# A graph-network kernel: prologue reordered, gathers three groups ahead, 32 instead of 20 rows left for the node stage

## The chip, the cores and the metric

The kernel runs on one core of a Trainium2 chip. The metric is the device time of one execution in microseconds (us), the median of several. A hardware profile of a single execution of the kernel before is used beside it. Engines are called as the profile calls them: PE (matrix products; PEld is its weight load), DVE (vector work), ACT (activations and copies), POOL (here the engine that issues the indirect DMAs), SP (here only an issuer of DMAs). "ACTq" and "SPq" stand for DMAs issued by those engines.

## What is computed

Two graph layers over 6250 nodes with 128 features and 100000 edges; `dst` is sorted, `src` is random.

```
radial = exp(coeff * (edge_weight - offsets)**2)                       # 50 per edge
h   = silu(concat(x[src], x[dst], radial) @ Wm1 + bm1)
h   = silu(h @ Wm2 + bm2);  messages = h @ Wm3 + bm3
out = segment_sum(messages, dst)
u   = silu(concat(x, out) @ Wu1 + bu1) @ Wu2 + bu2
x   = layernorm(x + silu(u @ Wi1 + bi1) @ Wi2 + bi2)

xt  = logmap0(x);  xs = xt[src]
att = sigmoid(concat(xs, xt[dst], edge_attr_128) @ att_w.T + att_b)
s   = xt + segment_sum(xs * att, src) + mean(edge_attr_128, src) + mean(edge_attr_128, dst)
out = layernorm(x + proj(expmap0(s)))
```

The means over `src` need every row of edge_attr_128 (100000 x 128) brought from the order of `dst` into the order of `src`.

## The kernel before

Edges go in 98 groups (`NG`) of 1024 edges; a group has 8 rows of 128 edges (b = 0 to 7), and two halves of 4 rows each. Nodes go in 49 blocks (`NB`) of 128. All of it is in `window_path` (L603).

**Prologue** (L874 to L1052). `x` is loaded in three chunks of blocks 0-8, 8-24 and 24-49, three SP DMAs each (L888 to L892). `src` and `dst` go into the tile `raw` by six DMAs from ACT's queue (L893 to L896). Small constants follow from POOL's queue (L897), then zero fills of table ends from SP (L900 to L902), and DVE clears `acc[:, 1]` (L903); DVE has cleared the end of `xs` before (L882). Then come two passes (`s` = 0 and 1) of 13 rounds of four node blocks (L1021). In pass 0 PE transposes `x` (L1014), ACT copies the result to SBUF (L1015), PE multiplies with the sources' part of Wm1 (L1033), DVE copies that to `pj_sb` (L1037), and SP writes it to the table `p_src` in HBM (L1044). Pass 1 does the same with the destinations' part for `p_dst`, and there ACT copies (L1039) and clears a piece of `acc` beside each of the first eight rounds (L1017). `pj_sb` has three buffers (L1030). Small pieces of index work (the list `pieces`, L992) are issued one a round from the fourth round of pass 0 on: turn `src` and `dst` to edge-per-partition form (`turn`, L928 to L930), the windows' bases (`bases`, `spread`, L941 to L953), positions relative to the bases (`relative`, L958, written to HBM at L960), high and low parts of the indices. What is left is issued after the rounds, then `lower(0)` and `lower(1)` (L989, L990; an ACT cast and a DMA from ACT's queue each). At the start of pass 1, SP issues the loads of groups 0 and 1 (L1023 to L1025).

**Edge stage** (L1282 to L1324). Each group needs 8 indirect DMAs by POOL that gather rows of `p_src` (`gather`, L1080, the DMA at L1087) into a tile `ga`, of which there are four (L836), and up to four loads of 64 rows of `p_dst` (`load_rows`, L1078, SP). The gathers of two groups are issued before the loop, and in the loop every half issues four of the group two further on (L1301). For each half, PE transposes the gathered rows and multiplies (L1204, L1207), ACT applies silu (L1210), PE and ACT do the second layer (L1219, L1221, L1223), PE sums the messages and the edge attributes by destination (L1236, L1238, L1240), and DVE adds to `acc` (L1252). DVE also works out, for each edge, its slot in a table ordered by source (`place`).

**Rows of edge_attr.** Rows 0, 1 and 2 of each group are scattered early into the table `early` by POOL's indirect DMAs (`scatter`, L816, the DMA at L818): two of the three rows of a group in the edge stage, straight after the half's gathers (L1302), as soon as ACT has written an index into the rows (L1324, the last thing of the group before). Row g % 3 of a group, the "third row", is always left for the node stage. `left(g)` (L550) names one more row to leave, in every fifth group, 20 in all; `early(g, half)` (L543) says which row a half scatters, if any. Rows 3 to 7 go in the attention stage.

**Node stage** (L1337 to L1473). The update of the nodes, 13 turns of four blocks. Beside it the left rows are moved: `middle` (L1337) holds 33 entries with the 98 third rows and 7 with the 20 left rows. `move_middle` (L1342) does one entry: load its rows again (SP, L1353), set an index by ACT (one copy for three rows at a constant stride, L1356, or one for each row, L1359), scatter them (POOL, L818). It is called three times in each of the 13 turns (L1425), and for the entries that are left after the turns (L1473). SP and POOL run in the order in which the program lists their work. The four tiles that it uses (L1353) are those that the first attribute loads of the attention stage use.

**Attention stage.** Summing by source (L1519 to L1829), with the late rows' scatters and the reads of the table `early` (`bucket_load`, L1590).

Of the kernel before, what the change touches and what calls it, by code (L numbers as in the profile page):

```python
# [8 lines left out]
F32 = mybir.dt.float32  # L9
I32 = mybir.dt.int32  # L10
AF = mybir.ActivationFunctionType
OP = mybir.AluOpType
# [4 lines left out]
P = 128  # L17
# [531 lines left out]

def left(g):  # L550

    return (1, 2, 0)[g % 3] if g % 5 == 0 else None

# [49 lines left out]
def window_path(ctx, tc, bad, x, src, dst, edge_attr, edge_weight, Wm1, bm1, Wm2, bm2, Wm3, bm3,  # L603
                Wu1, bu1, Wu2, bu2, Wi1, bi1, Wi2, bi2, att_w, att_b, out):
    nc = tc.nc
    ordered = ExitStack()
    ordered.enter_context(tc.manual_schedule())
    N, F = x.shape
    E = src.shape[0]
    NB = (N + P - 1) // P  # L610
    NFULL = N // P
    NREM = N - NFULL * P
    ROWS = 50 * P
# [3 lines left out]
    GE = 4 * WE  # L617
# [33 lines left out]
    row_rel = dram.tile([NG, GE], BF16, name="row_rel")  # L651


    const = ctx.enter_context(tc.tile_pool(name="const", bufs=1))
    ident = const.tile([P, P], F32, name="ident")
    make_identity(nc, ident)
# [34 lines left out]

    noff = const.tile([P, 1], F32, name="noff")
    nc.vector.tensor_scalar(noff, part, -float(KR), -STEP, op0=OP.add, op1=OP.mult)


    waiting = []
# [73 lines left out]
    later(attb, att_b[None, :].to_broadcast([P, 1]))  # L770


    keep = ctx.enter_context(tc.tile_pool(name="keep", bufs=1))

    src_i = sent.tile([P, 8, NG], I32, name="src_i")
    rel = sent.tile([P, 8, NG], F32, name="rel")
    hif = keep.tile([P, 2, 8, NG], F32, name="hif")
# [3 lines left out]
    first = sent.tile([P, 8, NG], F32, name="first")  # L781
    base_i = keep.tile([1, NG, 4], I32, name="base_i")
    badc = keep.tile([P, 1], F32, name="badc")
    acc = keep.tile([P, 3, ROWS], F32, name="acc")
    nc.vector.memset(ew3, 0.0)
    nc.vector.memset(badc, 0.0)

# [45 lines left out]

    of_edges = ExitStack()
    eload = of_edges.enter_context(tc.tile_pool(name="eload", bufs=2, reuse_waits="tile"))
    egat = of_edges.enter_context(tc.tile_pool(name="egat", bufs=4, reuse_waits="tile"))  # L836
    attrs, ids = {}, {}

    def extent(g):
# [34 lines left out]
    with tc.tile_pool(name="init", bufs=1) as init, \  # L874
            tc.tile_pool(name="initw", bufs=3) as initw, \
            tc.tile_pool(name="initp", bufs=2, space=PSUM) as initp:

        xs = acc[:, 0, :NB * F].rearrange("p (r f) -> p r f", f=F)
        xT = acc[:, 2, :NB * P].rearrange("f (r p) -> f r p", p=P)
        XL = N - (P - 1) * NB  # L880
        xv = x[:(P - 1) * NB].rearrange("(p r) f -> p r f", r=NB)
        nc.vector.memset(xs[96:, XL:], 0.0)  # L882
        raw = init.tile([NG, 2, GE], I32, name="raw")
        R0 = 96
        assert R0 == NG - 2 and NG * GE - E < GE
        nc.gpsimd.iota(raw[R0:, 0, TAIL:], pattern=[[1, GE - TAIL]], base=N, channel_multiplier=0)
        nc.vector.memset(raw[R0:, 1, TAIL:], -1)
        for lo, hi in ((0, 8), (8, 24), (24, NB)):  # L888
            nc.sync.dma_start(xs[:112, lo:hi], xv[:112, lo:hi])
            nc.sync.dma_start(xs[112:P - 1, lo:hi], xv[112:, lo:hi])  # L890
            nc.sync.dma_start(xs[P - 1:, lo:min(hi, XL)],
                              x[(P - 1) * NB + lo:(P - 1) * NB + min(hi, XL)][None])  # L892
        for s, v in enumerate((src, dst)):  # L893
            nc.scalar.dma_start(raw[:R0, s], v[:R0 * GE].rearrange("(g e) -> g e", e=GE))
            nc.scalar.dma_start(raw[R0:NG - 1, s], v[None, R0 * GE:(NG - 1) * GE])
            nc.scalar.dma_start(raw[NG - 1:, s, :TAIL], v[None, (NG - 1) * GE:])  # L896
        for f in waiting:  # L897
            f()
        for t in (p_src, p_dst):
            nc.sync.dma_start(t[NB * P:], zrow[:, :F])  # L900
        nc.sync.dma_start(first_t[(NB - 1) * LO:NB * LO].rearrange("(p r) f -> p r f", p=P),
                          zrow[:, None, :RW].to_broadcast([P, LO // P, RW]))  # L902
        nc.vector.memset(acc[:, 1], 0.0)  # L903


        rawf = init.tile([NG, 2, GE], F32, name="rawf")
# [11 lines left out]
        def turn(s):  # L918

            for h in range(2):  # L920
                pi = initp.tile([P, 4, P], F32, name="pi")
                for j in range(4):
                    k, c = divmod(4 * h + j, 2)
                    nc.tensor.transpose(
                        pi[:, j, :NG],
                        rawf[:, s].rearrange("g (k p c) -> g k c p", k=4, c=2)[:, k, c],
                        ident[:NG, :NG])
                nc.vector.tensor_copy((src_i, dst_i)[s][:, 4 * h:4 * h + 4], pi[:, :, :NG])  # L928
                if s:
# [32 lines left out]
        def upper(s):  # L962
            nc.vector.tensor_single_scalar(ti, (src_i, dst_i)[s], 7, OP.arith_shift_right)
            nc.vector.tensor_copy(hif[:, s], ti)
# [21 lines left out]
        def lower(s):  # L986
# [2 lines left out]
            nc.scalar.copy(rb, raw[:, s].rearrange("g (k p c) -> g k c p", k=4, c=2))  # L989
            nc.scalar.dma_start(row_lo[:, s], rb.rearrange("g k c p -> g (k c p)"))  # L990

        pieces = [  # L992
            lambda: nc.vector.tensor_copy(rawf[:, 0], raw[:, 0]),
            lambda: turn(0),
            lambda: nc.vector.tensor_copy(rawf[:, 1], raw[:, 1]),
            lambda: nc.vector.tensor_reduce(mx, dw, AX.X, OP.max),
            least,
            lambda: nc.vector.tensor_reduce(base, gone, AX.X, OP.min),
            bases, spread, relative, lambda: turn(1), lambda: upper(0), lambda: upper(1), rest, begins,
            lambda: bias_rows(init, bm2x, bm2p),  # L1000
            lambda: nc.vector.tensor_copy(beside[:, 1:], attw),
            copy_lws,
            lambda: nc.vector.tensor_single_scalar(raw, raw, P - 1, OP.bitwise_and)]


        tabs = [t[:NB * P].rearrange("(p r) f -> p r f", r=NB) for t in (p_src, p_dst)]
# [13 lines left out]
        turn_x(0)  # L1020
        for s in range(2):  # L1021
            if s:
                load(0)  # L1023
                load_attr(0)
                load(1)  # L1025
            for r, (b0, nb) in enumerate(rounds):
                if s == 0:
                    turn_x(r + 1)
                if r % 2 == 0:
                    pj_sb = initw.tile([P, 8, F], F32, name="pj_sb")  # L1030
                pj = initp.tile([P, 4, F], F32, name="pj")
                for i in range(nb):
                    nc.tensor.matmul(pj[:, i], lhsT=xT[:, b0 + i], rhs=wm1n[:, s],  # L1033
                                     start=True, stop=True)
                at = b0 % 8
                if s == 0:
                    nc.vector.tensor_copy(pj_sb[:, at:at + nb], pj[:, :nb])  # L1037
                else:
                    nc.scalar.copy(pj_sb[:, at:at + nb], pj[:, :nb])  # L1039
                    if r < 8:  # L1040
                        clear_sums.pop(0)()
                if r % 2 or r == len(rounds) - 1:
                    lo = b0 - at
                    nc.sync.dma_start(tabs[s][:, lo:lo + at + nb], pj_sb[:, :at + nb])  # L1044
                if s or r >= 3:
                    for _ in range(1):
                        if pieces:
                            pieces.pop(0)()
        for p_ in pieces:
            p_()  # L1050
        for s in range(2):
            lower(s)  # L1052

# [4 lines left out]
    with tc.tile_pool(name="ework", bufs=2, reuse_waits="tile") as ework, \  # L1058
# [3 lines left out]
            tc.tile_pool(name="eslot", bufs=1, reuse_waits="tile", space=PSUM) as eslot:  # L1062
        gas, feats, hots, hid1, hid2, sums, his = ({} for _ in range(7))

        counts = ework.tile([P, 2, NB], F32, name="counts", bufs=1)
        nc.vector.memset(counts, 0.0)
        befores = [ework.tile([P, 10, NB], BF16, name=f"before{i}", bufs=1) for i in range(2)]
# [12 lines left out]
        def gather(g, bs):  # L1080
            if g >= NG:
                return
            if g not in gas:
                gas[g] = egat.tile([P, 8, F], F32, name="ga")
            for b in bs:
                if b < 2 * windows(g):
                    nc.gpsimd.indirect_dma_start(  # L1087
                        out=gas[g][:, b], out_offset=None, in_=p_src[:, :],
                        in_offset=bass.IndirectOffsetOnAxis(ap=src_i[:, b, g:g + 1], axis=0))
# [189 lines left out]

        load_rows(0)  # L1280
        load_rows(1)
        for g in range(2):  # L1282
            gather(g, range(8))
        prepare(0, 0)
        rank(0)
# [3 lines left out]
        for g in range(NG + 2):  # L1289
            for half in range(2):  # L1290
                i = 2 * g + half
                if half == 0 and g + 2 < NG:
                    load_rows(g + 2)
                if half == 0 and g + 2 < NG:
                    load(g + 2)
                if half == 0 and g + 1 < NG:
                    load_attr(g + 1)

                if clear and i % 4 == 0:
                    nc.sync.dma_start(*clear.pop(0))  # L1300
                gather(g + 2, range(4 * half, 4 * half + 4))  # L1301
                if g < NG and early(g, half) is not None:  # L1302
                    scatter(g, early(g, half), attrs[g][0][:, early(g, half)])
                layer1(i)
                if i in extra:
                    extra[i]()
                layer2(i - 1)
                for f in clear_sums[:3]:
                    f()
                del clear_sums[:3]  # L1310
                add_up(i - 3)
                if g < NG and half == 0:
                    hot_of(g)
                if g + 1 < NG:
                    prepare(g + 1, half)
                    if half:
                        place(g + 1)
                if g < NG and half == 1:
                    weigh(g)
                sum_up(i - 2)  # L1320
                if g + 1 < NG and half == 0:
                    rank(g + 1)
                if g + 1 < NG and half == 1:
                    nc.scalar.copy(attrs[g + 1][0][:, :, F + 2], lof[:, :3, g + 1])  # L1324
# [548 lines left out]
```

## Time and profile before

| | |
|---|---|
| median of 6 runs | 2859.98 us (2857.42 to 2874.05) |
| the profiled execution | 2867.95 us, span 2866.1 us, mean granted PE clock 0.739 |
| PE / PEld busy | 1965.7 us (69%) / 1717.2 us (60%) |
| DVE busy | 1663.3 us (58%) |
| ACT busy | 914.2 us (32%) |
| POOL busy | 1528.1 us (53%) |
| DMA | 412.10 MB, mean 144 GB/s |
| gathers of `p_src` (L1087) | 782, 751.8 us busy, 961 ns each |
| early scatters in the edge stage (L818) | 176, 176.2 us busy, 1001 ns each |

The span is the profiled time from the first to the last recorded instruction; 1.9 us of the execution lie outside of it. In a list of instructions the columns are: start in us, duration in us, engine, line, operation, output<-input, shape, count, and in brackets the idle time of the engine before it and what ended that ("<-issue": nothing that the profile shows). In a table by stretches of time the columns are the stretch, its length, then the busy time and the number of instructions of PE, PEld, DVE, ACT and POOL, the granted PE clock (1.00 is full), the share of the DMA engines that was busy, and GB/s.

### The profile page before, as it was taken

The page shows a single profiled execution, that of the slowest core. Times are in us where ns is not written, and L with a number is a line of the kernel's source. Part 1 is how long each engine was busy: PE and PEld are TensorE (multiplying, and loading weights), DVE is VectorE, ACT ScalarE, POOL GpSimd, SP SyncE. Part 2 cuts the span into 40 slices and gives each one's busy share as a digit, 9 for nine tenths or more (in the row PEclk, how much of TensorE's full clock was granted, in tenths as well). Part 3 has the DMA queues.
Part 4 walks back from the last instruction along what each step waited for, and adds up shares of the span by engine and source line. Part 5 has one row for each costly group of instructions (what it writes and reads, how often), then busy time and mean ns, then how long its engine had stood idle before and what let it go on. Part 6 is the DMA issues. An engine that isn't in the chain of part 4 may idle for free. (4 is left out here: it accounts for less than half of the span.)

```text
span 2866.1 us, 41631 instructions
## 1 busy us (share of the span) xinstructions
PE 1965.7 (69%) x13313; PEld 1717.2 (60%) x13317; DVE 1663.3 (58%) x4460; ACT 914.2 (32%) x1576; POOL 1528.1 (53%) x1598
## 2 busy tenths in 40 slices
PE   5677667766767577777777786656666777677763
PEld 5566556665656566666666673425656677666663
DVE  5656646566565656665665662354544555565668
ACT  2544434444444344444444431121111110000005
POOL 4455555555555555565655536445555556555530
PEclk8778778877878777787778786656665666676776
DMA  6445435444544444444433433336566766666743
GB/s 198 125 125 139 131 94 134 132 117 114 134 132 110 116 119 127 116 125 119 108 99 99 111 84 101 103 118 190 183 194 207 213 207 216 208 222 206 252 136 86
DMA packets 349796, 412.10 MB, mean 144 GB/s; under 512 B 53749, under 2 KB 265979, under 8 KB 349313
## 3 DMA queue, kind: packets, MB, share of 16 engines
q1 hardware_dynamic: 298216, 303.00, 37.2%
q0 software_dynamic: 50624, 105.02, 12.3%
q8 instruction: 108, 1.77, 0.3%
q10 hardware_dynamic: 728, 1.33, 0.2%
q14 instruction: 120, 0.98, 0.1%
HBM read 319.13 MB, written 90.00 MB: 143 GB/s over the span
## 5 line engine op out<-in xcount | busy, mean ns | idle before, releaser
L1087 POOL DMA_INDIRECT ga<-p_src,src_i x782 | 751.8, 961 | 260.4 <-issue 230.8
L1252 DVE TENSOR_TENSOR acc<-acc,ps 128x192 f32 x391 | 138.1, 353 | 518.4 <-remote 264.8
L818 POOL DMA_INDIRECT early<-attr_row,to_i x176 | 176.2, 1001 | 490.0 <-ACT attr_row L1324 247.2
L1619 PE MATMUL pb<-acc,oh 128*128 128x130 f32 x1960 | 395.9, 381 | 47.7 <-issue 41.0
L818 POOL DMA_INDIRECT late<-attr,to_i x298 | 289.6, 972 | 257.3 <-ACT att L1692 155.1
L1619 PEld LDWEIGHTS pb<-acc,oh 128*128 128x128 f32 x1960 | 372.6, 289 | 55.8 <-issue 53.9
L1236 PE MATMUL ps<-hot,h 128*128 128x64 f32 x1564 | 323.4, 285 | 72.7 <-issue 71.5
L1210 ACT ACTIVATE h<-pa,bm1c 128x512 f32<-128x512 f32 x196 | 134.6, 687 | 649.0 <-remote 230.2
L1221 PEld LDWEIGHTS pb<-wm,h 128*128 128x128 f32 x1564 | 269.4, 242 | 87.3 <-issue 64.5
L1207 PE MATMUL pa<-feat,lw 128*128 128x256 f32 x782 | 283.0, 491 | 46.7 <-issue 41.5
L1236 PEld LDWEIGHTS ps<-hot,h 128*128 128x128 f32 x1564 | 268.1, 212 | 70.4 <-issue 69.1
L1221 PE MATMUL pb<-wm,h 128*128 128x128 f32 x1564 | 265.3, 323 | 30.9 <-issue 30.7
L1677 PE MATMUL pg<-a,ohT 128*128 128x49 bf16 x2346 | 124.4, 200 | 208.8 <-DVE ohT L1663 173.1
L1686 DVE TENSOR_TENSOR pick<-pg,hi 128x416 f32<-128x416 f32 x98 | 57.8, 590 | 348.3 <-PE pb L1619 210.6
L1238 PE MATMUL ps<-hot,attr 128*128 128x64 f32 x976 | 205.2, 287 | 61.6 <-issue 61.3
L1677 PEld LDWEIGHTS <-ohT 128*128 128x128 bf16 x2346 | 107.0, 106 | 234.4 <-DVE ohT L1663 192.4
L1207 PEld LDWEIGHTS pa<-feat,lw 128*128 128x128 f32 x782 | 179.1, 252 | 81.2 <-issue 61.3
L1204 PE MATMUL pa<-ident,ga 128*128 128x128 f32 x782 | 163.4, 329 | 91.0 <-issue 57.1
L1238 PEld LDWEIGHTS ps<-hot,attr 128*128 128x128 f32 x976 | 162.7, 205 | 66.6 <-issue 66.4
L1223 ACT ACTIVATE h<-pb 128x512 f32<-128x512 f32 x196 | 116.4, 594 | 238.4 <-remote 102.4
L1204 PEld LDWEIGHTS pa<-ident,ga 128*128 128x128 f32 x782 | 113.9, 171 | 110.9 <-issue 77.0
L1689 ACT ACTIVATE attr<-lg,attb 128x5 f32<-128x5 f32 (+1 forms) x60 | 18.2, 304 | 441.7 <-DVE lg L1688 440.1
(339 smaller groups left out, 3946.1 us busy)
## 6 DMA issues: line engine op xcount, KB each, us to landing
los<-row_lo SPq DMA_DIRECT2D x98, 512.0 KB
near<-in_edge_weight_dram SPq DMA_DIRECT2D x97, 256.0 KB
attr<-in_edge_attr_dram SPq DMA_DIRECT2D x97, 256.0 KB
acc<-late SPq DMA_DIRECT2D x44, 528.0 KB
late<-zrow SPq DMA_DIRECT2D x22, 792.0 KB
acc<-early SPq DMA_DIRECT2D x49, 330.0 KB
attr<-in_edge_attr_dram SPq DMA_DIRECT2D x247, 64.0 KB
attr<-in_edge_attr_dram SPq DMA_DIRECT2D x118, 128.0 KB
```

The lines of the kernel that those rows point to most:

```text
L818: nc.gpsimd.indirect_dma_start(out=t, out_offset=bass.IndirectOffsetOnAxis(ap=to_i[:, b, g:g + 1], axis=0), in_=rows_, in_offset=None)
L1087: nc.gpsimd.indirect_dma_start(out=gas[g][:, b], out_offset=None, in_=p_src[:, :], in_offset=bass.IndirectOffsetOnAxis(ap=src_i[:, b, g:g ...
L1204: nc.tensor.matmul(pa[:, j], lhsT=gas[g][:, 2 * k0 + j], rhs=ident, is_transpose=True, start=j == 0, stop=False)
L1207: nc.tensor.matmul(pa[:, 2 * k:2 * k + 2], lhsT=lws[(4 * g + k0 + k) % NL], rhs=feats[g][:, k0 + k], start=False, stop=k == kk - 1)
L1210: nc.scalar.activation(hid1[i][:, :2 * kk], pa[:, :2 * kk], AF.Silu, bias=bm1c)
L1221: nc.tensor.matmul(pb[:, j], lhsT=h1[:, j], rhs=wm2, start=False, stop=j == nb - 1)
L1223: nc.scalar.activation(hid2[i][:, :nb], pb[:, :nb], AF.Silu)
L1236: nc.tensor.matmul(ps[:, k, 0], lhsT=h2[:, 2 * k + c], rhs=hot[:, b], start=k == 0 and c == 0, stop=False)
L1238: nc.tensor.matmul(ps[:, k, 1], lhsT=head[:, b, :F] if b < 3 else rest[:, b - 3], rhs=hot[:, b], start=False, stop=False)
L1252: nc.vector.tensor_add(acc[:, :, bass.ds(at, W)], acc[:, :, bass.ds(at, W)], ps[:, k])
L1619: nc.tensor.matmul(pb[:, h], lhsT=oh[:, a + h, j], rhs=bt[:, a + h, j, :S], start=j == 0 and h == 0, stop=j == c - 1 and h == n - 1)
L1677: nc.tensor.matmul(pg[:, b, :NB], lhsT=ohT[:, 0, b], rhs=a3[q], start=q == 0, stop=q == 2)
```

## The change

1. `left(g)`: a second row is left in the groups with g % 9 equal to 0, 4 or 8 (32 of the 98 groups) instead of every fifth. The early scatters of the edge stage go from 176 to 164, and the scatters of the node stage from 118 to 130 (44 entries in place of 40).
2. Gathers run three groups ahead, with six `ga` tiles instead of four; three groups are gathered before the loop.
3. The tile `acc` is made first, and the clearing of the end of `xs` becomes DVE's first work; `acc[:, 1]` is cleared before the loads are issued. ACT gets a small copy (`here`) near its start.
4. `src` and `dst` are loaded from SP's queue, in the order x chunk 0, x chunk 1, `src`, x chunk 2, `dst`.
5. The pieces are in two lists: seven in pass 0, up to `bases`; the others in pass 1. `lower(0)` and `lower(1)` are issued in rounds 5 and 8 of pass 1, the loads of groups 0 and 1 in its rounds 9 and 11.

```diff
-    return (1, 2, 0)[g % 3] if g % 5 == 0 else None
+    return (1, 2, 0)[g % 3] if g % 9 in (0, 4, 8) else None
...
+    keep = ctx.enter_context(tc.tile_pool(name="keep", bufs=1))
+    acc = keep.tile([P, 3, ROWS], F32, name="acc")
...
+    nc.vector.memset(xs[96:, XL:], 0.0)
...
+    here = const.tile([P, 1], F32, name="here")
+    nc.scalar.copy(here, part)
...
-    egat = of_edges.enter_context(tc.tile_pool(name="egat", bufs=4, reuse_waits="tile"))
+    egat = of_edges.enter_context(tc.tile_pool(name="egat", bufs=1, reuse_waits="tile"))
+    ga_tiles = [egat.tile([P, 8, F], F32, name=f"ga{i}") for i in range(4)]
...
-        nc.vector.memset(xs[96:, XL:], 0.0)
...
-        for lo, hi in ((0, 8), (8, 24), (24, NB)):
+        nc.vector.memset(acc[:, 1], 0.0)
+        for i, (lo, hi) in enumerate(((0, 8), (8, 24), (24, NB))):
             nc.sync.dma_start(xs[:112, lo:hi], xv[:112, lo:hi])
...
-        for s, v in enumerate((src, dst)):
-            nc.scalar.dma_start(raw[:R0, s], v[:R0 * GE].rearrange("(g e) -> g e", e=GE))
-            nc.scalar.dma_start(raw[R0:NG - 1, s], v[None, R0 * GE:(NG - 1) * GE])
-            nc.scalar.dma_start(raw[NG - 1:, s, :TAIL], v[None, (NG - 1) * GE:])
+            if i:
+                v = (src, dst)[i - 1]
+                nc.sync.dma_start(raw[:R0, i - 1], v[:R0 * GE].rearrange("(g e) -> g e", e=GE))
+                nc.sync.dma_start(raw[R0:NG - 1, i - 1], v[None, R0 * GE:(NG - 1) * GE])
+                nc.sync.dma_start(raw[NG - 1:, i - 1, :TAIL], v[None, (NG - 1) * GE:])
...
-        nc.vector.memset(acc[:, 1], 0.0)
...
-            bases, spread, relative, lambda: turn(1), lambda: upper(0), lambda: upper(1), rest, begins,
+            bases], [
+            spread, relative, lambda: nc.vector.tensor_single_scalar(raw, raw, P - 1, OP.bitwise_and),
+            lambda: turn(1), lambda: upper(0), lambda: upper(1), rest, begins,
             lambda: bias_rows(init, bm2x, bm2p),
-            lambda: nc.vector.tensor_copy(beside[:, 1:], attw),
-            copy_lws,
-            lambda: nc.vector.tensor_single_scalar(raw, raw, P - 1, OP.bitwise_and)]
+            lambda: nc.vector.tensor_copy(beside[:, 1:], attw), copy_lws]]
...
             if s:
-                load(0)
                 load_attr(0)
-                load(1)
             for r, (b0, nb) in enumerate(rounds):
+                if s and r in (9, 11):
+                    load(r // 2 - 4)
+                if s and r in (5, 8):
+                    lower(r // 3 - 1)
...
-                if s or r >= 3:
-                    for _ in range(1):
-                        if pieces:
-                            pieces.pop(0)()
-        for p_ in pieces:
-            p_()
-        for s in range(2):
-            lower(s)
+                if pieces[s] and (s or r >= 3):
+                    pieces[s].pop(0)()
+            assert not pieces[s]
...
+        ga_tiles += [ework.tile([P, 8, F], F32, name=f"ga{i}", bufs=1) for i in (4, 5)]
...
-                gas[g] = egat.tile([P, 8, F], F32, name="ga")
+                gas[g] = ga_tiles[g % len(ga_tiles)]
...
-        for g in range(2):
+        for g in range(3):
             gather(g, range(8))
...
-                gather(g + 2, range(4 * half, 4 * half + 4))
+                gather(g + 3, range(4 * half, 4 * half + 4))
```

More of the change, by code (lines that the diff above doesn't have):

```diff
@@ L651, in window_path @@
     row_rel = dram.tile([NG, GE], BF16, name="row_rel")
+    keep = ctx.enter_context(tc.tile_pool(name="keep", bufs=1))
+    acc = keep.tile([P, 3, ROWS], F32, name="acc")
+    xs = acc[:, 0, :NB * F].rearrange("p (r f) -> p r f", f=F)
+    XL = N - (P - 1) * NB
+    nc.vector.memset(xs[96:, XL:], 0.0)
     const = ctx.enter_context(tc.tile_pool(name="const", bufs=1))
@@ L770, in window_path @@
     later(attb, att_b[None, :].to_broadcast([P, 1]))
-    keep = ctx.enter_context(tc.tile_pool(name="keep", bufs=1))
     src_i = sent.tile([P, 8, NG], I32, name="src_i")
@@ L783, in window_path @@
     badc = keep.tile([P, 1], F32, name="badc")
-    acc = keep.tile([P, 3, ROWS], F32, name="acc")
     nc.vector.memset(ew3, 0.0)
@@ L876, in window_path @@
             tc.tile_pool(name="initp", bufs=2, space=PSUM) as initp:
-        xs = acc[:, 0, :NB * F].rearrange("p (r f) -> p r f", f=F)
         xT = acc[:, 2, :NB * P].rearrange("f (r p) -> f r p", p=P)
-        XL = N - (P - 1) * NB
         xv = x[:(P - 1) * NB].rearrange("(p r) f -> p r f", r=NB)
-        nc.vector.memset(xs[96:, XL:], 0.0)
         raw = init.tile([NG, 2, GE], I32, name="raw")
@@ L990, in lower @@
             nc.scalar.dma_start(row_lo[:, s], rb.rearrange("g k c p -> g (k c p)"))
-        pieces = [
+        pieces = [[
             lambda: nc.vector.tensor_copy(rawf[:, 0], raw[:, 0]),
```

## The prediction

> **What bounds the kernel now.** I read first the table of busy times by stretches, cut where the trace changes character.
>
> ```profile
> 43.00:84.00 41.00, 13.44 (x67) 11.26 (x67) 12.97 (x48) 14.22 (x22) 23.40 (x24) 0.60 0.51 161
> 84.00:1690.00 1606.00, 1142.44 (x6815) 999.97 (x6818) 983.72 (x2848) 718.34 (x876) 902.32 (x932) 0.78 0.45 119
> 1690.00:1909.00 219.00, 153.23 (x545) 92.17 (x544) 81.11 (x266) 38.01 (x105) 116.41 (x120) 0.69 0.33 97
> ```
>
> No engine fills the edge stage (84 to 1690): PE has 1142 of 1606 us. So I looked in the lists of POOL and PE at where one group's time goes.
>
> ```profile
> 644.85 0.95 POOL L1087 DMA_INDIRECT ga<-p_src,src_i  x1 [0.31 <-issue]
> 649.30 1.00 POOL L818 DMA_INDIRECT early<-attr_row,to_i  x1 [3.50 <-ACT attr_row L1324]
> ...
> 665.72 0.95 POOL L1087 DMA_INDIRECT ga<-p_src,src_i  x1 [0.30 <-issue]
> 671.16 1.00 POOL L818 DMA_INDIRECT early<-attr_row,to_i  x1 [4.50 <-ACT attr_row L1324]
> ```
>
> ```profile
> 656.99 0.39 PE L1238 MATMUL ps<-hot,attr 128*128 128x64 f32 x2
> ...
> 661.07 0.22 PE L1238 MATMUL ps<-hot,attr 128*128 128x64 f32 x1 [1.80 <-issue]
> ...
> 667.47 0.37 PE L1204 MATMUL pa<-ident,ga 128*128 128x128 f32 x1 [2.48 <-issue]
> ...
> 669.84 1.91 PE L1207 MATMUL pa<-feat,lw 128*128 128x256 f32 x4
> ```
>
> POOL takes its DMAs one every 1.255 us (0.95 and 0.30 between) until the scatter of a half 0, which waits for ACT's copy of L1324, the last work of the group before. So POOL goes in runs: usually scatter, 4 gathers, scatter, 4 gathers, 10 in 12.3 us; the run shown, 649.30 to 666.67, has 14. PE keeps pace until some 8 us into the run; then it gets single instructions after gaps of 1.0 to 2.5 us put down to "issue", and goes on 2 to 3 us after the run's last DMA (666.67; PE at full pace from 669.6). Of the runs that I followed, those of 9 and more mostly show this, those of 5 don't. Then the loop closes: PE late, ACT's copy late, POOL's next run late. A group thus costs **POOL's run and about 4 us**. From the start of a run to that of the next: 16.54 us (59 runs of 10), 21.6 (12 of 14), 12.0 (13 of 5), 16.3 (6 of 9, 14.6 to 18.4).
>
> The opening is one such run:
>
> ```profile
> 42.65 1.08 POOL L1087 DMA_INDIRECT ga<-p_src,src_i  x1 [21.45 <-DVE hif L964]
> ...
> 72.47 0.94 POOL L1087 DMA_INDIRECT ga<-p_src,src_i  x1 [0.30 <-issue]
> 88.05 1.14 POOL L818 DMA_INDIRECT early<-attr_row,to_i  x1 [14.63 <-ACT h L1210]
> ```
>
> ```profile
> 64.23 0.59 ACT L1039 COPY pj_sb<-pj 128x512 f32<-128x512 f32 x1 [6.48 <-remote]
> 76.20 0.59 ACT L1039 COPY pj_sb<-pj 128x512 f32<-128x512 f32 x1 [11.38 <-remote]
> ```
>
> 24 gathers stand in 42.65 to 73.41, and meanwhile the rounds of p_dst, 1.25 us apart before, come 6.5 and 11.4 us apart. They resume at 76.2, 2.8 us after the run, and the edge stage's first transpose (L1204) is at 84.0.
>
> **The prologue.** In pass 0 x's last chunk (issued 9.06 to 12.4) reaches PE at 24.28 only, and the last copy of pass 0 is at 38.97, 14.7 us later. The change moves dst's 0.39 MB and fills of 0.46 MB behind it; at the 207 GB/s of the first 43 us that is 4.1 us, and SP's 1.3 us wait for DVE's clearing goes: landing near 19 (18 to 21). The six DMAs leave ACT's queue (ACT's first copy comes at 12.94, its table load at 11.65), but src's three now queue on SP ahead of x's last chunk; that is in the 21. `spread` (1.41 us) and `relative` (1.20) leave pass 0, where DVE is the pacer: 14.7 - 2.0 = 12.7. Last copy 31.7, first gather **35.3 instead of 42.65**. DVE's 5.39 us clearing moves under the loads, where DVE idles; without that cover it delays the first copy as now, at no loss.
>
> The opening run now has 32 gathers: 32 x 1.265 = 40.5, so it ends at 75.8 instead of 73.4, and PE is free near 78.6 instead of 76.1. `lower` (two casts of 1.09 us and two issues, 77.83 to 80.8) leaves the tail, of which I count half: edge stage **+1 us** (-8 if landing and tail both go well, +4 if x's chunk lands at 21 and the tail saves nothing). The gain of 7.3 us is eaten by 8 gathers of 10.1.
>
> The Trainium skill ("DMA: Bandwidth & Descriptors", section "Issuing engines are not separate DMA queues") says that all queues run on the same 16 DMA engines and that spreading issues saves only issue time. By it nothing is won by which engine issues, only by order; that would be the 4.1 us without the 1.3, an edge start 1 us later again.
>
> **Gathers three groups ahead.** Directly this is worth little: PE waits for `ga` in 10.2 us of the edge stage (7 waits). I take 0 (0 to -10). But the loop has one group fewer to gather for. The last two groups, without gathers, took 10.7 and 12.0; a third saves 16.5 - 12.0 = **-4.5**.
>
> **32 rows left.** Which half loses its scatter decides how runs join. Now 13 pairs of runs 14 + 5 (33.6 us against 2 x 16.54: +0.5 each) and 6 of nine (-0.2 each): +5.3. After it, groups 8 and 9 of each nine both lose the scatter that stops POOL: 14, 9, 5 in a row, ten times. A nine lasts 11.1 us; with the 4.2 us that follow a run of ten (16.54 - 12.3) it costs 15.3: 21.6 + 15.3 + 12.0 = 48.9 against 49.6, -0.7 each. Eleven single nines: -0.2 each. Together -9.2, and against +5.3 now **-14.5**. With nines at 14.6 or at 18.4 instead of 15.3 the triples give -7 or +31 more: -21 to +16; I lean to the low side since the mean of six is 16.3. Twelve early scatters fewer are 15 us of POOL, which agrees with the size. Edge stage together -19, rounded **-18**.
>
> **The node stage** has 44 entries instead of 40. The 13 turns take 39 both times; after them stand 5 entries with 14 scatters instead of 1 with 2.
>
> ```profile
> 1905.49 0.97 POOL L818 DMA_INDIRECT early<-attr_last,to_i  x1 [0.31 <-issue]
> 1931.10 0.97 POOL L818 DMA_INDIRECT late<-attr,to_i  x1 [24.64 <-DMA los<-row_lo]
> ```
>
> 12 x 1.275 = 15.3 us on POOL, which idles 24.64 us there: it ends at 1921.8 instead of 1906.5. Queued behind on SP are 12 row loads, then the read of `early` (L1590, at 1908.14 now), which needs the last scatter landed. PE, held until about 2.4 us after the run (1924.2), has its products L1519 at 1918.2 now: 6 us late. I take **+7** (0 if PE isn't held, +17 with the loads and 12 ACT copies paid in full).
>
> **Sum:** +1 - 18 + 7 = **-10**. The profiled execution took 2867.95 us (span 2866.1, 1.9 outside), 8 above the median of 2859.98; so about 2858 for such a one and **2850** for the median. 0.3% is 8.6 us, about what a measurement of this kernel can tell from no change: faster is below 2851.4, slower above 2868.6.
>
> A rule that speaks against the main step: the gaps on PE are single-instruction gaps without a semaphore, and they end with POOL's run. The Trainium skill ("Runtime: NRT & Kernel Launch", section "Instruction fetch mechanics") lets the sequencer refill its instructions in blocks of 16 KiB by a DMA queue of its own, at a cost "mostly hidden". By it the gaps wouldn't follow POOL's runs, the pattern of runs would be worth nothing, and the sum would be -4.5 + 1 + 7 = +4.
>
> **Rivals.** *B, slower:* the left rows are only carried over. If periods depend on work per group and not on how runs join, -14.5 becomes 0, while the tail costs its 15.3 and the prologue +3: -4.5 + 15.3 + 3 = +14, **2874**. It decides once POOL's last early scatter (1921.8) and PE's release pass 1919, when PE's L1526 and the weights for L1663 (1926.76) start. For it: the idle gap has a chain on DVE, 17 of 22 us busy. Against it: runs of 14 and 5 differ so regularly (21.0 to 21.9; 9.2 to 13.3).
> *C, the opening run doesn't hold PE* (the copies wait for p_dst's own writes, as one 5.21 us wait at 52.04 does): then pass 1 runs at 1.25 us a round, 31.9 + 16.3 = 48.2, and with 6.3 us of tail (77.67 to 84.0) and slower writes the edge stage starts near 57, 27 us sooner. The same disbelief takes away the -14.5: -27 - 4.5 + 7 = -24, **2835**. Against it: 11.38 us at 76.20 "remote", just after the run's end.
> *D, it doesn't do what it says:* x's chunk lands as late as now (queued behind src on SP). First gather at 42, eight gathers more: +10 instead of +1: **2859**, no change.
>
> **Chances.** Forecast 0.50 (own range 2836 to 2866: six tenths of it faster, a third the same), B 0.22, C 0.14, D 0.14. Faster 0.30 + 0.14 = 0.44; same 0.17 + 0.14 = 0.31; slower 0.03 + 0.22 = 0.25. The range reaches from C's far side to B's price: 2826 to 2876.
>
> **What would show it.** First gather near 35, last opening gather near 76, L1204 first near 85 (C: 57). In the edge stage runs of 14, 9, 5 with about 21.6, 15.3, 12.0 between starts, and some 18 us less until the last L1252; equal periods for every group of work would show B. The stretch from the node stage's start to the first late scatter (1690 to 1931.10 now) 7 us longer, and 12 more early scatters in a row at its end. The attention stage unchanged (851 us). I am wrong if PE's gaps stay in number and length though the runs change.

## The result, and the profile after

The changed kernel takes **2894.7 us** (median of 20 runs, 2866.74 to 2912.67); the kernel before, run beside it, 2857.78 us (46 runs). The ratio is **1.0121, interval 1.0099 to 1.0142**: some 35 us slower, where -10 was forecast and 2876 was the end of the range. The profiled execution of the change took 2878.37 us (span 2876.4), 16 below its own median, while that of before lay 8 to 10 above its; so the two profiles show 10 us of the 35, and I read from them where the time went, not how much. One thing matters for what follows: in the last three sets of experiments the kernel before took 2167 us. I call that B, and where it takes some 2860 us A. The sets of runs name their chip by number: 0 and 10 for A, 0 and 11 for B, so it isn't shown that A and B are two chips and not one in two conditions. Every ratio compares runs of one set.

By landmarks of the two traces (A), in us:

| | before | after |
|---|---|---|
| first gather, end of the opening run | 42.65, 73.41 | 39.92, 81.97 |
| first product with `lw` (L1207, now L1212) | 84.85 | 92.62 |
| from there to the last addition to `acc` (L1252, now L1257) | 1623.4 | 1652.0 |
| from there to the first late scatter | 222.9 | 214.1 |
| from there to the end | 935.0 | 917.7 |

The loss is in the edge stage (+28.7) and ahead of it (+7.8). The two last rows went the other way (-8.8 and -17.3). Stretches of the trace after, cut at the same landmarks as those of before:

```profile
40.00:92.00 52.00, 14.02 (x88) 11.92 (x86) 21.63 (x71) 16.16 (x24) 33.73 (x33) 0.62 0.45 135
92.00:1727.00 1635.00, 1145.69 (x6808) 1005.90 (x6812) 976.73 (x2837) 718.09 (x874) 883.02 (x911) 0.79 0.43 116
1727.00:1936.00 209.00, 143.41 (x548) 88.24 (x548) 80.23 (x263) 38.39 (x115) 119.34 (x123) 0.72 0.36 104
```

PE, ACT and the clock do what they did (1146 us, 718 us, 0.79; before 1142, 718, 0.78); POOL has 19 us less to do; still the stretch is longer. The time is in waits. First the opening, POOL, then ACT and PE after the change:

```profile
39.92 2.53 POOL L1092 DMA_INDIRECT ga<-p_src,src_i  x1 [14.95 <-DMA attr_row<-in_edge_attr_dram]
...
81.02 0.95 POOL L1092 DMA_INDIRECT ga<-p_src,src_i  x1 [0.30 <-issue]
90.73 1.20 POOL L826 DMA_INDIRECT early<-attr_row,to_i  x1 [8.76 <-ACT attr_row L1293]
```

```profile
74.22 0.59 ACT L1048 COPY pj_sb<-pj 128x512 f32<-128x512 f32 x1 [16.96 <-remote]
86.83 0.75 ACT L1048 COPY pj_sb<-pj 128x512 f32<-128x512 f32 x2 [12.02 <-remote]
```

```profile
76.19 1.06 PE L1209 MATMUL pa<-ident,ga 128*128 128x128 f32 x4
92.62 2.05 PE L1212 MATMUL pa<-feat,lw 128*128 128x256 f32 x4 [15.38 <-DMA lw<-p_dst]
```

The first gather is 2.7 us sooner, not 7.3; the opening run is 8 gathers longer; and the last copies for p_dst again come only once it is over (86.83, 4.9 us behind its end). The first transpose of gathered rows, forecast near 85, was at 76.19, but the product behind it waited 15.38 us for rows of p_dst.

Then the runs in the edge stage, POOL after the change, with the lines at which a run begins and ends:

```profile
671.31 1.00 POOL L826 DMA_INDIRECT early<-attr_row,to_i  x1 [3.68 <-ACT attr_row L1329]
...
687.72 0.95 POOL L1092 DMA_INDIRECT ga<-p_src,src_i  x1 [0.30 <-issue]
694.44 0.99 POOL L826 DMA_INDIRECT early<-attr_row,to_i  x1 [5.76 <-issue]
...
704.72 0.95 POOL L1092 DMA_INDIRECT ga<-p_src,src_i  x1 [0.30 <-issue]
711.73 0.99 POOL L826 DMA_INDIRECT early<-attr_row,to_i  x1 [6.06 <-ACT h L1215]
...
723.72 0.99 POOL L826 DMA_INDIRECT early<-attr_row,to_i  x1 [5.77 <-issue]
```

Runs of 14, 9 and 5 are there as foreseen, and every DMA is as long and as close to the next as before (0.95 and 0.30). But the nine costs 17.3 us here, not 15.3, and the three together 52.4, not 48.9. All such runs of the trace: 22.1 (9 of 14), 16.8 (19 of 9), 12.8 (11 of 5), and those of 10 take 16.84 (49) where they took 16.54.

PE's waits, before, after, and then with nothing but the tiles made by hand (an experiment below), over the edge stage (us in total, times, longest):

```profile
PE ps L1236 <- issue: 71.5, 88, 2.5
PE ps L1238 <- issue: 69.8, 86, 2.6
```

```profile
PE ps L1241 <- issue: 108.7, 121, 2.6
PE ps L1243 <- issue: 106.5, 132, 2.5
```

```profile
PE ps L1239 <- issue: 113.6, 133, 2.5
PE ps L1237 <- issue: 102.4, 109, 2.5
```

These are the single-instruction gaps, in the same two products; both groups grew by half. Not all of that is lost: other products had fewer gaps, and all idle time of PE's products put down to "issue" went from 326 us to 363 after the change and 372 with the tiles alone. The change without such tiles has 350, the left rows alone 338.

### The profile page after: what moved, and what is told of

It is laid out like the page before. It is cut to its first block, busy times and chain, and to the rows that moved or that the text cites. A ratio compares the mean times of both kernels' runs of the same rounds, so it can differ in the third digit from the quotient of the medians.

```text
span 2876.4 us, 42310 instructions
## 1 busy us (share of the span) xinstructions
PE 1956.1 (68%) x13313; PEld 1716.1 (60%) x13317; DVE 1658.5 (58%) x4460; ACT 915.3 (32%) x1589; POOL 1530.2 (53%) x1598
## 3 DMA queue, kind: packets, MB, share of 16 engines
q8 instruction: 108, 1.77, 0.3%
## 5 line engine op out<-in xcount | busy, mean ns | idle before, releaser
L1257 DVE TENSOR_TENSOR acc<-acc,ps 128x192 f32 x391 | 138.0, 353 | 543.1 <-remote 353.3
L826 POOL DMA_INDIRECT early<-attr_row,to_i x164 | 163.9, 1000 | 537.7 <-ACT attr_row L1329 204.9
L1212 PE MATMUL pa<-feat,lw 128*128 128x256 f32 x782 | 288.5, 500 | 60.1 <-issue 40.1
L1226 PEld LDWEIGHTS pb<-wm,h 128*128 128x128 f32 x1564 | 263.0, 236 | 71.1 <-issue 46.6
L1243 PE MATMUL ps<-hot,attr 128*128 128x64 f32 x976 | 213.1, 290 | 94.2 <-issue 92.3
L1226 PE MATMUL pb<-wm,h 128*128 128x128 f32 x1564 | 259.5, 318 | 25.1 <-issue 22.1
L1682 PE MATMUL pg<-a,ohT 128*128 128x49 bf16 x2346 | 116.0, 198 | 210.4 <-DVE ohT L1668 196.0
L1212 PEld LDWEIGHTS pa<-feat,lw 128*128 128x128 f32 x782 | 182.4, 257 | 94.8 <-issue 71.6
L1243 PEld LDWEIGHTS ps<-hot,attr 128*128 128x128 f32 x976 | 168.5, 210 | 91.3 <-issue 91.0
L1228 ACT ACTIVATE h<-pb 128x512 f32<-128x512 f32 x196 | 116.3, 593 | 178.4 <-PE pb L1226 55.7
```

The costliest lines, as they stand in the source:

```text
L826: nc.gpsimd.indirect_dma_start(out=t, out_offset=bass.IndirectOffsetOnAxis(ap=to_i[:, b, g:g + 1], axis=0), in_=rows_, in_offset=None)
L1212: nc.tensor.matmul(pa[:, 2 * k:2 * k + 2], lhsT=lws[(4 * g + k0 + k) % NL], rhs=feats[g][:, k0 + k], start=False, stop=k == kk - 1)
L1226: nc.tensor.matmul(pb[:, j], lhsT=h1[:, j], rhs=wm2, start=False, stop=j == nb - 1)
L1228: nc.scalar.activation(hid2[i][:, :nb], pb[:, :nb], AF.Silu)
L1243: nc.tensor.matmul(ps[:, k, 1], lhsT=head[:, b, :F] if b < 3 else rest[:, b - 3], rhs=hot[:, b], start=False, stop=False)
L1257: nc.vector.tensor_add(acc[:, :, bass.ds(at, W)], acc[:, :, bass.ds(at, W)], ps[:, k])
```

## The experiments

"Gaps" below is a sum that I worked out from each trace: steps from one PE or PEld start to the next of 0.6 to 0.8, 1.25 to 1.55 or 2.0 to 2.25 us, lengths taken from the single-instruction gaps, between 90 and 1700 us. Before: 421 us, of which 372 end by "issue". After: 456. The sum doesn't rank the kernels: it is 429 with the tiles alone, which cost 38 us, and 444 with the left rows alone, which are a gain.

### The parts alone (A)

**The pattern of left rows alone**, the kernel before with:

```diff
-    return (1, 2, 0)[g % 3] if g % 5 == 0 else None
+    return (1, 2, 0)[g % 3] if g % 9 in (0, 4, 8) else None
```

> The kernel before with the new pattern of left rows alone (32 instead of 20), everything else as before. Theory J (how POOL's runs join costs the time): in the profile after, runs of 14, 9 and 5 in a row take 22.1 + 16.8 + 12.8 = 51.7 us against 49.6 for three runs of 10, ten times, while the 13 pairs of before cost 0.5 each, so +21 - 6 = +15 us, up to +25 with the 12 scatters more in the node stage. Theory A (gathering three groups ahead costs it): 0 to +5 us. Theory P (the prologue costs it): 0.

Measured: 0.9965 (0.9934 to 0.9996), -10 us. Theory J falls: this part is a gain.

**Gathers three groups ahead alone**, as in the change (four `ga` tiles made by hand in `egat`, two in `ework`, `range(3)`, `gather(g + 3, ...)`).

> The kernel before with six ga tiles, three groups gathered before the loop and group g + 3 gathered in it, left rows and prologue as before. Theory J: the opening run has 8 gathers more (+10 us at the start of the edge stage) and the loop one group fewer (-4.5): about +5 us. Theory A: +20 us or more, the runs of 10 lasting longer than 16.5 us each. Theory P: 0 to +5.

Measured: 1.0082 (1.0048 to 1.0117), +23 us. Theory A has its number.

**The prologue alone.** I made this kernel from the changed one, setting `range(3)`, `g + 3`, the six tiles and the left rows back; the four tiles stayed made by hand.

> The kernel before with the new prologue alone (loads, clearings, pieces); two groups gathered before the loop, left rows as before. Theories J and A: the first gather comes 2.7 us sooner and the opening run has 24 gathers as before, so -3 us (edge stage starting at 82 instead of 85). Theory P (pass 1 of the prologue loses more than the opening run explains): +8 us, the edge stage starting near 92 again.

Measured: 1.0105 (1.0061 to 1.0149), +30 us. The edge stage started at 82.8, 2 us sooner than before, and lasted 1654.7 us instead of 1623.4. That fits none of the three theories: what computes or moves data in the stage is that of before in the same order, and it took 31 us longer.

**The change with the old pattern of left rows:**

> The changed kernel with the old pattern of left rows (20). Theory J: only the prologue's 8 us and the group fewer are left, +3 to +10 us against the kernel before. Theory A: +25 to +35 us, as the whole change. Theory P: +8 us.

Measured: 1.0035 (1.0003 to 1.0066), +10 us. Theory A falls here; theory J has its number, but it fell above.

What the three slower ones share, and the faster one has not, stands in POOL's program. Two stretches of it, each DMA with the semaphores that it waits for, before and with tiles made by hand:

```
L1087 DMACopy ga<-p_src,src_i [waits DMASW4,PE]
L1087 DMACopy ga<-p_src,src_i [waits DMASW5]
L1087 DMACopy ga<-p_src,src_i [waits DMASW6]
L1087 DMACopy ga<-p_src,src_i [waits DMASW7]
...
L1088 DMACopy ga_201<-p_src,src_i [waits DMASW0,PE]
L1088 DMACopy ga_201<-p_src,src_i [waits DMASW1,PE]
L1088 DMACopy ga_201<-p_src,src_i [waits DMASW2,PE]
L1088 DMACopy ga_201<-p_src,src_i [waits DMASW3,PE]
```

A tile from the rotating pool is given back as a whole: its first gather waits for PE, seven don't. A tile made once is tracked row by row: each gather waits for PE's transpose of its own row. In this program a DMA carries one wait itself, and what it waits for beyond that stands in instructions ahead of it: 656 more on POOL with four such tiles, 645 in the changed kernel. They wait for a transpose of two or three groups ago; the traces show no DMA held up by it (below).

### The tiles made by hand (A)

**Nothing but the tiles**, the kernel before with:

```diff
-    egat = of_edges.enter_context(tc.tile_pool(name="egat", bufs=4, reuse_waits="tile"))
+    egat = of_edges.enter_context(tc.tile_pool(name="egat", bufs=1, reuse_waits="tile"))
+    ga_tiles = [egat.tile([P, 8, F], F32, name=f"ga{i}") for i in range(4)]
...
-                gas[g] = egat.tile([P, 8, F], F32, name="ga")
+                gas[g] = ga_tiles[g % len(ga_tiles)]
```

> The kernel before, but its four ga tiles made once and taken in turn by hand, as the change does it, instead of from a rotating pool; nothing else. The instructions that compute or move data are the same in the same order; POOL gets 640 instructions more that only wait on a semaphore. Theory W (these waits cost the time): the runs with hand-made tiles gave +23, +30, +10 and +35 us, those without -10; solved as a sum the tiles alone are worth +43, so +25 to +45 us. Theory S (the start of the edge stage sets the pattern in which POOL's runs and PE's work meet, and that moves the time either way): within 10 us of before.

Measured: **1.0132 (1.0076 to 1.0188), +38 us**. Theory W has its number; S had 10 at most.

**The whole change without them:**

```diff
-                gas[g] = ga_tiles[g % len(ga_tiles)]
+                gas[g] = (egat.tile([P, 8, F], F32, name="ga") if g % 6 < 4 else
+                          ework.tile([P, 8, F], F32, name="ga", bufs=2))
```

> The changed kernel with its six ga tiles from two rotating pools (four and two buffers), so that POOL's additional waits are gone; all else as changed. Theory W: 35 to 45 us less than the changed kernel: 2850 to 2860, level with before or below. Theory S: 2895 as the changed kernel, or anywhere between.

Measured: **0.9980 (0.9942 to 1.0019)**, 2857.47 us: by the ratios 40 us less than the changed kernel, and level with before.

**The prologue alone, and three groups ahead alone, with rotating tiles:**

> The new prologue alone once more, but with the rotating pool of before (the run of the prologue alone above carried hand-made tiles over from the change). Theory W: -15 to 0 us against before. Theory S: +30 us as that run.

> Gathers three groups ahead alone once more, with six tiles from two rotating pools. Theory W: -20 to +5 us against before (the run with hand-made tiles gave +23). Theory S: +23 us.

Measured: 0.9976 (0.9944 to 1.0007), -7 us, and **0.9961 (0.9928 to 0.9994)**, -11 us. Four kernels with rotating tiles lie 6 to 11 us below before (two of the four intervals include no change); five with tiles by hand, the changed one among them, 10 to 38 us above. Four pairs differ in the tiles alone: 38 us on the kernel before, 40 in the change, 37 with the prologue (+30 against -7), 34 with the gathers (+23 against -11). The edge stage in the tiles alone, and then in the change without them:

```profile
85.00:1726.00 1641.00, 1137.02 (x6824) 997.26 (x6826) 985.20 (x2855) 720.80 (x878) 902.36 (x932) 0.79 0.43 116
```

```profile
92.00:1689.00 1597.00, 1124.80 (x6810) 986.70 (x6814) 980.56 (x2836) 717.43 (x875) 881.08 (x911) 0.80 0.44 119
```

With the tiles alone POOL's work is that of before to 0.1 us (902.36 against 902.32, cut at the same landmarks) in a stretch 35 us longer. The runs are those of before, 59 of 10, 12 of 14, 13 of 5 and 6 of 9, but the first three kinds take 16.90, 22.25 and 12.35 us from start to start where they took 16.55, 21.60 and 11.98: that is 33 us in all. In the runs of 10, PE and PEld got 116.3 of their instructions started from a run's start to 2 us after its end, against 120.7 before; 18 of 59 took over 17 us, against 12.

### How waits that are over can cost time (B)

Two doses and two tests of the gaps. They were meant for A and came to run on B, also when they were repeated.

**Two tiles by hand, two rotating** (334 additional waits), and all four again beside it:

> The kernel before with two of its four ga tiles made by hand and two from a rotating pool: 320 to 330 additional waits on POOL instead of 640 to 656. Theory W (each additional wait costs its share): half of the +39 us of all four, +12 to +28. If it is not the number of the waits but that the tiles are made by hand at all (their places, or one late wait): 0 or +39.

> Two of four tiles by hand: 334 additional waits. If the number of waits counts, half of what the run beside it (all four by hand) shows: +12 to +28 where that is +39. If only the fact counts that tiles are made by hand: the same +39. If phases of the loop decide, not the waits: anything from -10 to +40, not between the two by rule. On a chip without the gaps 0, as measured.

> The kernel before with four hand-made ga tiles, once more, to stand beside the next run. Where the kernel before takes some 2860 us: +39 us as measured (22 to 54). Where it takes some 2167 us and PE has no single-instruction gaps, POOL's DMAs follow each other without a pause and set the time of the edge stage: if the additional waits lengthen no DMA and no pause, 0 (+-3); if each wait costs POOL 60 ns always, +39 there too.

Measured on B: half 1.0003 (0.9992 to 1.0014) and 1.0002 (0.9992 to 1.0013), all 1.0008 (0.9998 to 1.0019). All four tiles by hand cost **2 us here, at most 4**, where they cost 38 on A. So a wait has no fixed price: 656 at 38 us would be some 58 ns each. Whether on A it is the number of the waits, or something else about tiles made by hand, such as their places, stays open: the runs that were to tell came to B.

**Half of the gathers left out** (so the messages aren't the reference's), and **gathers paced by half groups**:

```diff
-                if b < 2 * windows(g):
+                if b < 2 * windows(g) and b % 4 < 2:
...
-                nc.tensor.matmul(pa[:, j], lhsT=gas[g][:, 2 * k0 + j], rhs=ident, is_transpose=True,
+                nc.tensor.matmul(pa[:, j], lhsT=gas[g][:, 2 * k0 + j % 2], rhs=ident, is_transpose=True,
```

```diff
...
+                    if b % 4 == 0:
+                        gas[g, b // 4] = egat.tile([P, 4, F], F32, name="ga")
...
-                gather(g + 2, range(4 * half, 4 * half + 4))
...
                 layer1(i)
+                gather(g + 2, range(4 * half, 4 * half + 4))
```

> The kernel before with only rows 0, 1, 4 and 5 of each group gathered, and PE using them also for rows 2, 3, 6 and 7 (it leaves out half of the gathers, so the messages are not the reference's); PE, DVE and ACT do the same work as before. Theory R (POOL's run of indirect DMAs holds PE once it has lasted some 8 us): the run of 10 becomes one of 6, 7.5 us, without single-instruction gaps on PE, and a group takes some 12 to 12.5 us as after the runs of 5: 98 x 4.2 = 350 to 420 us less. Rival (the gaps belong to PE's own instruction stream): the gaps stay at some 420 us in all, and at most the 12 us are saved that PE waits for gathered rows.

> Half of the gathers left out, PE using rows 0, 1, 4 and 5 also for 2, 3, 6 and 7 (so the messages are not the reference's). Theory R (POOL's run of more than some 8 us makes PE's gaps): runs of 6, the gaps gone, 350 to 420 us less where the kernel before takes 2860 us. Rival (the gaps come from elsewhere and only happen to be seen beside POOL's runs): the gaps keep some 420 us, at most 30 us less. On a chip without gaps 70 us less as measured, POOL no longer setting the time.

> Half of the gathers left out once more (the messages are not the reference's). Where the kernel before takes some 2860 us: theory R says the gaps are gone and 350 to 420 us less; the rival, gaps of some 420 us still, at most 30 us less. Where it takes some 2167 us: 70 us less as twice measured.

> The kernel before with ga tiles of half a group from a rotating pool of four, and the gathers of group g + 2 put behind layer 1 of the half whose tile they take over, so that POOL stops at every half for PE: runs of at most 5 in place of runs of 10 with the same DMAs in all. Theory R with the count starting anew at each pause: hardly a gap on PE, a group in 12.6 us (POOL's ten DMAs) to 14 us: 250 to 380 us less. If short pauses don't end it: 16.5 us a group and no gain; if POOL's stops make it late for its own scatters: slower by up to 100 us.

> Gathers paced by half groups, at most 5 DMAs without a stop. Theory R with the count starting anew at each pause: 250 to 380 us less where the kernel before takes 2860 us. If short pauses don't end the gaps: about 0, or up to 100 us slower. On a chip without gaps +9 us as measured.

Measured on B: half of the gathers 0.9669 (0.9654 to 0.9684), 0.9681 (0.9667 to 0.9695), 0.9654 (0.9626 to 0.9681), 69 to 75 us less (the edge stage 1126 us, 11.5 a group); paced 1.0039 (1.0024 to 1.0055) and 1.0049 (1.0032 to 1.0066). On B there is nothing for them to take away, as this stretch of POOL shows (two tiles by hand, its second run on B; such a kernel is within 0.1% of before there, and stands for it below):

```profile
604.23 0.99 POOL L818 DMA_INDIRECT early<-attr_row,to_i  x1 [0.30 <-issue]
...
610.54 0.99 POOL L818 DMA_INDIRECT early<-attr_row,to_i  x1 [0.30 <-issue]
...
616.87 0.99 POOL L818 DMA_INDIRECT early<-attr_row,to_i  x1 [0.30 <-issue]
```

and its waits for gathered rows and its page (the same kernel):

```profile
PEld pa L1205 <- DMA ga<-p_src,src_i: 131.2, 105, 5.4
...
PE pa L1205 <- DMA ga<-p_src,src_i: 102.4, 83, 5.2
```

```profile
PE 1665.7 (77%) x13313; PEld 1471.9 (68%) x13317; DVE 1665.0 (77%) x4460; ACT 920.2 (42%) x1576; POOL 1545.4 (71%) x1598
```

The scatter of a half 0 finds its data ready, POOL goes on without a pause (in its first run on B for 1182 us), a group takes its ten DMAs, 12.6 us, and PE waits for gathers. The sum of gaps gives 64 us, but those in the edge stage all end by a DMA or by DVE: PE's products have 0.2 us of idle time put down to "issue" there, where the kernel before has 326 on A. So **POOL's uninterrupted runs alone don't make the gaps**; whether they do on A, what the two tests were for, is not answered.

**The change on B.** Its first part, prologue and gathers with rotating tiles and 20 left rows, and then the changed kernel itself:

> The changed kernel with rotating tiles and the old pattern of 20 left rows: prologue and three groups ahead without the additional waits. If the parts add up (-7 for the prologue, -11 for the gathers): -18 us against before, and the pattern of left rows is worth +12 in this company (the changed kernel with rotating tiles and 32 rows left was -6). If the parts don't add up: -5 to -10, and the pattern is worth nothing.

> The changed kernel once more. Where the kernel before takes some 2860 us: +35 us as measured. Where it takes some 2167 us: there POOL's DMAs set the time of the edge stage, 1.27 us each; 12 early scatters fewer in it and 8 gathers moved ahead of it are 15 + 10 us less, 8 gathers more in the opening +10 us if PE waits for them, 12 scatters more at the end of the node stage 0 to +15 us, the waits +2: -15 to +5 us. If the waits cost there as well: +35.

Measured: 0.9979 (0.9968 to 0.9990), -5 us, and **0.9928 (0.9907 to 0.9950), -16 us** (-15 to +5 was expected): here the change is faster. The edge stage with two tiles by hand, then with the change:

```profile
66.00:1264.00 1198.00, 987.67 (x6942) 882.74 (x6945) 998.90 (x2904) 729.28 (x888) 906.48 (x940) 0.90 0.61 160
```

```profile
64.00:1244.00 1180.00, 983.82 (x6945) 875.13 (x6945) 998.89 (x2888) 722.39 (x888) 895.37 (x929) 0.91 0.61 162
```

POOL sets the time here. Its first gather comes 1.3 us sooner (40.4 against 41.7) and it has 12 scatters fewer (12 x 1.27 = 15 us); the stage starts 1.5 us sooner and ends 20 us sooner. From its end to the first late scatter it takes 170.8 us instead of 163.6.

## Why the prediction was wrong

**The step that failed** is that on the gathers three groups ahead, "Directly this is worth little". It priced the transfers and not the edit that holds them, the `ga` tiles taken out of the rotating pool. By itself that costs 38 us (22 to 54) on A, and the change is 40 us shorter without it; the forecast missed by 45. The part for which it says "I take 0 (0 to -10)" and -4.5 measured +23 alone with these tiles and -11 with rotating ones. The diff showed the edit, and the range had no term for it.

**The prologue: +1, measured +7.8** in the trace. x's last chunk reached PE at 22.00, not 19 (24.28 before), and from there to the last copy of pass 0 it took 14.0 us (14.7 before), not 12.7. "The gain of 7.3 us is eaten by 8 gathers of 10.1" was 2.7 against 11.3 (32 gathers in 42.05 us, where 24 took 30.76). That the opening run holds p_dst back agrees with both traces on A; no run there tests it. On B it doesn't: there (two tiles by hand) the last copies come at 58.0 and 58.5, in the middle of the opening run of 41.7 to 72.7, and the first transpose at 64.8; with the change they come at 54.3 and 54.8, and the transpose at 58.2, near the 57 of rival C.

**The left rows: -14.5 and +7, measured -10** (-19 to -1) alone: the right sign and size, as far as shown by luck. The working is not borne out: it priced a nine at 15.3 though the six nines in the trace took 16.3, which by the same sum makes the three runs 49.9 and no gain. The kernel with this pattern alone shows 21.6 + 16.0 + 12.3 = 49.9 for 14, 9 and 5, and 49 runs of 10 at 16.7. What the 10 us are made of was not settled.

**The node stage: +7**, measured -9 in the trace after, +1 with the left rows alone (223.6 us against 222.9), +7 on B. On A single traces can't tell: six kernels that keep the 20 rows show 210.5 to 224.5 us there beside the 222.9 of before. POOL's last early scatter did move behind the last turn (1947.4, 11.6 us after the update of x; before it was 2.3 us ahead), and it was covered.

**The sum** of -10 is near what the change is without these tiles, -6 (-17 to +5) on A, though its terms came out otherwise (and -14.5 with -4.5 is -19, not -18). On B, against the kernel with two tiles by hand, the terms came out as -1.5, -18 and +7, with -5 for the rest of the trace, where the forecast had +1, -18, +7 and 0. The -18 agrees for another reason: POOL's own work sets that stage there. The parts don't add up on A: -7, -11 and -10 alone, -6 together.

**Rival B** had the side, not the size (2874, +14 where +35 was measured) nor the cause: its pattern alone is faster, and its tail is covered. **D** was half right: the first gather, priced at 35.3 and by D at 42, came at 39.92.

**"POOL's run and about 4 us"** was read off one trace and described it; as a law it fails on B, where POOL never stops and PE's products have 0.2 us of such gaps. The rule that I weighed against it (the Trainium skill, "Runtime: NRT & Kernel Launch", section "Instruction fetch mechanics") calls the cost of such a refill "mostly hidden". By it the gaps would be no matter of instruction fetch. The instruction queue q8 moves the same 108 packets, 1.77 MB in all, in the trace of before and in that of two tiles by hand on B, 56 of them in the edge stage of each, with 333 such idle times of PE's products in the one and a single one in the other: the number of fetches isn't what differs, and no run here shows more of the rule than that. What makes the gaps on A, and by what way tiles made by hand cost time there, **stays open**.

## What to carry to other kernels

Price a change of buffers like a change of work: list, for the engine that refills them, how many waits an instruction has before and after; here tiles held by hand are followed piece by piece, tiles from a rotating pool are given back as a whole. When parts are tried alone, compare the programs engine by engine first: the first "prologue alone" carried the tiles along and pointed the wrong way. And look at the time of the base kernel in every set of runs: the same change is 1.2% slower on A and 0.7% faster on B, so a verdict holds for the bound that was there. The change with rotating tiles was level with before on A (0.9980); on B it was run with 20 left rows only (0.9979).

## What the hardware showed that I had not expected

The same program takes 2860 us on A and 2167 on B. Stage by stage (on B two tiles by hand): the edge stage 1623 and 1198 us, first to last late scatter 838 and 642, the mean granted clock 0.74 and 0.85. DVE, ACT and POOL are busy for nearly the same time on both (1663 and 1665, 914 and 920, 1528 and 1545 us), PE for 1966 and 1666. On A PE's products lose 326 us of the edge stage to idle time that ends by nothing the profile shows, most of it in steps of 0.7 and 1.4 us, on B 0.2.

The half clock comes behind idle time: in the trace of before the granted clock is 0.5 for 43% of the edge stage; 4 us after the middle of these gaps it is 0.5 for 92% of them (counted by time), 4 us before their middle for 12%. After PE's other waits there it is 82%, and on B, where 0.5 takes 19% of the stage, 65%. So the lower clock is no ready cause of the gaps. That it makes them cost a second time, in PE's busy time (1142 us in the edge stage, 988 on B), fits but isn't tested.

And tiles made by hand, with 656 more instructions on POOL that only wait, cost 38 us on A, though no DMA of POOL got longer by it (968 ns, and 305 ns between two, with and without), and 2 us on B.
